# Two places for the queries, half a score tile ahead over ends of blocks, and one place for elu's exponential and h

## The chip, the cores and the metric

The kernel runs on one core of a Trainium2 chip. Its time is the device time of one execution in microseconds (us). Before the change it is 4391.52 us, the median of three executions (4390.94 to 4396.86).

The engines of a core work side by side, each through its own queue in order: TensorE (PE in the profile, its weight loads PEld), VectorE (DVE), ScalarE (ACT), GpSimd (POOL) and SyncE (SP). In this kernel every DMA is issued from SP's queue.

## The reference

Two layers over x of shape (8, 2048, 256), with one adjacency matrix of 2048 x 2048. Layer 0 is attention with 4 heads of 64, whose softmax is taken within each chunk of 256 keys, then an output projection with a residual and a layer norm. Layer 1 is a graph attention whose weights come from two scores per node. Each layer's output is added to its input and normalised. Cut to what matters:

```python
q, k, v = (x @ W.T + b for each)                     # 4 heads of 64
scores = clip(q @ kc.T / 8, -10, 10)                 # for each chunk of 256 keys
scores = where(adj == 0, -10, scores)
ctx = sum over chunks of softmax(scores) @ vc
h = layernorm(x + layernorm(ctx @ Wo.T + bo + x) * gamma + beta)
# layer 1
Wh = h @ W;  e = leaky_relu(Wh @ a1 + (Wh @ a2).T, 0.2)
p = softmax(where(adj > 0 or diagonal, e, -inf))
out = layernorm(h + elu(p @ Wh))
```

## The kernel before, in words

**Blocks, chunks, beats.** Layer 0 works on *blocks* of 512 queries of one batch: 8 batches x 4 blocks = 32. A block goes through 8 *chunks* of 256 keys (j), a chunk through two *beats* (half 0 and 1) of 128 keys, whose number within the block is c (0 to 15). The loop over J (256 chunks and one more) writes out the work of all engines in the order in which each engine's queue will hold it.

**A beat.** The scores of 128 keys and 4 heads are two *halves* (hp), each a tile `sc` of 128 x 1024 in PSUM: four matmuls in the profile (L882), one clip with the mask's cap on VectorE (L893), one exponential on ScalarE (L897) into a tile e. Then come the context's matmuls of the chunk before (L948): in half 0 the sums (weights `ones`) and the first part of the values, in half 1 the second part. Each ends in a tile m of two places in PSUM, which ScalarE copies out (ds L962, un L956). The sums go over SP: dc<-ds (L964), a reciprocal on VectorE (L970), rd<-dc (L972), r<-rd (L976). Two beats later VectorE scales un by r (L983) and POOL adds it to ctxT (L984).

**Halves ahead.** `sc` has two places of its own. While layer 1 is not under way (`spare`), its accumulator's place `us` serves as a third, and each beat multiplies and clips the first half of the *next* beat as well (`todo`, L922 to L933, kept in `ahead_sc`); the next beat begins with its exponential. Before the change this stops at a block's last beat (`c + 1 < NT`).

**Queries.** qT, the block's projected queries, has one place. x's transposed block xT_q is loaded (512 KB, L120) at the end of chunk 6 of the block before (`j == NCH - 2`). At the end of chunk 7 `make_qT` projects it: 8 matmuls pq in the profile (L256) in two m tiles, evicted by ScalarE (L257).

**Ends of beats.** `end_beat` writes out layer 1's products (L746), then one step of each generator: `ahead` (a batch's prelude of layer 1, with pw L398, psj L416, the maxima L438 and pab L461) and `fins`. The latter hold the keys' and values' projections (pk L256, pv L275), in batch 0 the masks (mk L154 and L155, mb L157, mf L201), `fin` (the output of a layer 0 block: x is loaded, po L357, two layer norms, h stored, transposed by pt L383) and `fin1` (the end of a layer 1 block). Then the agenda's reciprocals and scalings. A generator's `yield` ends its share of the beat.

**Layer 1.** Steps of 128 keys run beside layer 0, 1.5 to a beat: w in five places through ScalarE (L714), VectorE (L718, L723), ScalarE (L727), then its products and on POOL the sum acc (L734, L736). They start a few chunks into a batch, when the prelude is done, so every batch has a stretch without them; batch 0 has none at all.

**fin1.** It loads h (hr, 512 KB, L591), divides by the sums (L597 to L601), takes the exponential ex (L603), builds elu (L605, VectorE), adds hr (L606, POOL), and normalises (`stats`, `normalize`, L611). hr and ex have a place of 4 KB per partition each. `fin1_last` does the same for the last batch, with its own ex. The place of hr also serves un in some chunks of batch 0.

Of the kernel before, what the change touches and what calls it, by code (L numbers as in the profile page):

```python
# [9 lines left out]
F32 = mybir.dt.float32  # L10
# [9 lines left out]
P = 128  # L20
# [8 lines left out]
def tile_adj_attention__then__gat(  # L29
# [35 lines left out]
    nc = tc.nc  # L65
    B, N, F = x.shape
    H, D = 4, 64
    CHUNK = 256
    KC = F // P
    NT = N // P  # L70
    IB = 512
    NIB = N // IB
    TPB = IB // P
    NPAIR = H // 2
    NCH = N // CHUNK
    DH = D // 2
    HT = NT // 2
    HN = N // 2
    QSCALE = 1.0 / D**0.5
# [38 lines left out]
    def xT_tile(b, ib, name):  # L118
        t = four.tile([P, KC, IB], F32, tag="xT", name=f"xT_{name}{b}_{ib}")
        nc.sync.dma_start(out=t, in_=xT[b, :, ts(ib, IB)].rearrange("(k p) n -> p k n", p=P))  # L120
        return t
# [5 lines left out]
    bq_c = load_c("bq_c", bq)  # L127
# [99 lines left out]
    nc.sync.dma_start(out=W_aug[:, :, 0:F], in_=W.rearrange("(k p) o -> p k o", p=P))  # L227
    a_bc = []
    for n in range(2):
        t = one.tile([P, F], F32, tag=("hx", "ex")[n], name=f"a_bc{n}")  # L230
        nc.sync.dma_start(out=t, in_=a[n * F : (n + 1) * F, :].rearrange("f o -> (f o)").partition_broadcast(P))
        a_bc.append(t)

# [17 lines left out]
    def proj_T(dst, name, xt, bias, scale, tag):  # L251

        for o in range(NPAIR):
            pm = ps_m.tile([P, IB], F32, tag="m", name=f"p{tag}_{o}")
            for k in range(KC):
                nc.tensor.matmul(pm, WT[name][:, k, ts(o, P)], xt[:, k, :], start=(k == 0), stop=(k == KC - 1))  # L256
            nc.scalar.activation(dst[:, o, :], pm, AF.Identity, bias=bias[:, o : o + 1], scale=scale)  # L257
# [26 lines left out]
    def projections():  # L284


        for b in range(B):
            first = (b * NIB - 1) * 2 * NCH
            for n in range(NIB):
# [13 lines left out]
                    yield  # L303
                make_v(b, n)

    def make_qT(b, ib, xt):
        qT = one.tile([P, NPAIR, IB], F32, tag="qT", name=f"qT{b}_{ib}")
        proj_T(qT, "q", xt, bq_c, QSCALE, f"q{b}_{ib}")
        return qT

    def stats(src, name):

# [274 lines left out]

    def fin1(b, ib, hx, acc):

        hr = one.tile([P, TPB, F], F32, tag="hr", name=f"hr{b}_{ib}")  # L590
        nc.sync.dma_start(out=hr, in_=h_d[b, ib])  # L591
        yield


        pr = ps_m.tile([P, TPB], F32, tag="m", name=f"pr{b}_{ib}")
        for t in range(TPB):
            nc.tensor.matmul(pr[:, t : t + 1], acc[:, ts(t, P)], ones[:, 0:1], start=True, stop=True)  # L597
        r = two.tile([P, TPB], F32, tag="r1", name=f"r1{b}_{ib}")
        nc.vector.reciprocal(r, pr)
        for t in range(TPB):  # L600
            nc.scalar.activation(hx[:, t, :], hx[:, t, :], AF.Identity, bias=ones[:, 0:1], scale=r[:, t : t + 1])  # L601
        ex = one.tile([P, TPB, F], F32, tag="ex", name=f"ex{b}_{ib}")
        nc.scalar.activation(ex, hx, AF.Exp, bias=shifts[:, 1:2])  # L603
        yield
        nc.vector.scalar_tensor_tensor(hx, ex, 1.0, hx, ALU.min, ALU.max)  # L605
        nc.gpsimd.tensor_add(hx, hx, hr)  # L606
        yield
        mv, rstd = yield from stats(hx, f"c{b}_{ib}")
        yield
        normalize(hx, mv, rstd, f"c{b}_{ib}")  # L610
        nc.sync.dma_start(out=out[b, ts(ib, IB), :].rearrange("(t p) f -> p t f", p=P), in_=hx)  # L611

    def fin1_last(b, ib, hx):


        hr = one.tile([P, TPB, F], F32, tag="hr", name=f"hr{b}_{ib}")
        nc.sync.dma_start(out=hr, in_=h_d[b, ib])
        ex = one.tile([P, TPB, F], F32, tag="ex", name=f"ex{b}_{ib}")
        st = two.tile([P, TPB, 6], F32, tag="st", name=f"st_c{b}_{ib}")
        mv = two.tile([P, TPB, 2], F32, tag="mv", name=f"mv_c{b}_{ib}")  # L620
        rstd = two.tile([P, TPB], F32, tag="rstd", name=f"rstd_c{b}_{ib}")
        nmr = two.tile([P, TPB], F32, tag="nmr", name=f"nmr_c{b}_{ib}")
        ends = ib == NIB - 1

        def exponential(r):
            nc.scalar.activation(ex[:, r, :], hx[:, r, :], AF.Exp, bias=shifts[:, 1:2])

        def elu(r):
            nc.vector.scalar_tensor_tensor(hx[:, r, :], ex[:, r, :], 1.0, hx[:, r, :], ALU.min, ALU.max)

# [12 lines left out]
        def scale(t):  # L643
            nc.scalar.activation(
                hx[:, t, :], hx[:, t, :], AF.Identity, bias=nmr[:, t : t + 1], scale=rstd[:, t : t + 1]
            )

        def store(r):
            n = (r.stop - r.start) * P
            q0 = ib * IB + r.start * P  # L650
            nc.sync.dma_start(out=out[b, q0 : q0 + n, :].rearrange("(t p) f -> p t f", p=P), in_=hx[:, r, :])

        halves = [slice(0, 2), slice(2, 4)]
        if ends:
# [12 lines left out]
        yield  # L667
        for r in halves:
            exponential(r)
            yield  # L670
            elu(r)
        yield
        for r in halves:
            add(r)
            yield
        for t in range(TPB):
            tile_stats(t)
            yield
        spread_of(slice(0, TPB))
        yield  # L680
        for r in halves:
            for t in range(r.start, r.stop):
                scale(t)
            yield
        store(slice(0, TPB))
# [176 lines left out]
    blocks0 = {(0, 0, 0): first_m0}  # L862
    make_kT(0, 0)
    make_mask(0, first_m0, first_raw, 0, 0, 0, 2)
    qT = make_qT(0, 0, xT_kv[0, 0])
    fins.append(projections())
    fins.append(weights_made())
    fins.append(masks_made())
# [3 lines left out]
    halves_done = 0  # L872
    ahead_sc = None

    def scores(n, hp):

        nonlocal halves_done
        pool, tag = (ps_u, "us") if spare and halves_done % 3 == 2 else (ps_s, "sc")
        halves_done += 1
        sc = pool.tile([P, 2, IB], F32, tag=tag, name=f"sc{b}_{ib}_{n}_{hp}")  # L880
        for h in range(2):
            nc.tensor.matmul(  # L882
                sc[:, h, :],
                kTs[b][n // TPB][h * D : (h + 1) * D, hp, ts(n % TPB, P)],
                qT[h * D : (h + 1) * D, hp, :],
                start=True,
                stop=True,
            )
        return sc

    def clip(sc, n):
        cap = blocks0[b, ib, n // HT][:, n % HT, :].unsqueeze(1).to_broadcast([P, 2, IB])
        nc.vector.scalar_tensor_tensor(sc, sc, -CLIP, cap, ALU.max, ALU.min)  # L893

    def exponentials(chunk, n, hp, sc):
        e = eight.tile([P, 2, IB], F32, tag="e", name=f"e{b}_{ib}_{n}_{hp}")
        nc.scalar.activation(e, sc, AF.Exp)  # L897
        chunk["es"].append(e)

    for J in range(total + 1):  # L900
# [5 lines left out]
        for half in range(2):  # L906
# [11 lines left out]
            if live:  # L918


                spare = not (l1_open() or leaking)
                todo = [(c, hp) for hp in range(0 if ahead_sc is None else 1, NPAIR)]  # L922
                if spare and c + 1 < NT and (b, ib, c + 1) != (0, 0, HT):
                    todo.append((c + 1, 0))
                scs = [scores(n, hp) for n, hp in todo]
                for (n, hp), sc in zip(todo, scs):
                    clip(sc, n)
                ahead_sc = None
                for (n, hp), sc in zip(todo, scs):
                    if n == c:  # L930
                        exponentials(cur, c, hp, sc)
                    else:
                        ahead_sc = sc  # L933
            middle_of_beat()
# [60 lines left out]
            end_beat()  # L995
            if half == 1:

                if live and j == NCH - 2 and J + 2 < total:
                    nb, nib = (b, ib + 1) if ib + 1 < NIB else (b + 1, 0)
                    xq = xT_tile(nb, nib, "q")  # L1000
                if live and j == NCH - 1 and J + 1 < total:
                    qT = make_qT(nb, nib, xq)
            beat += 1
        prev = cur if live else None

# [49 lines left out]
```

## Time and profile before

| what | value |
|---|---|
| median of three executions | 4391.52 us |
| the profiled execution | 4386.54 us |
| its span, first to last instruction | 4384.7 us |
| mean granted TensorE clock | 0.979 |
| TensorE busy | 4055.8 us |
| VectorE busy | 3417.1 us |
| ScalarE busy | 2555.5 us |
| GpSimd busy | 1759.3 us |
| pq matmuls (248 and 8 more in the first block) | 115.8 and 3.6 us busy |
| scores, L882 (4096) | 1038.7 us busy |
| clips, L893 (1024) | 1205.8 us busy, 1.222 us each |

The profile comes from one execution. Its page gives busy times of engines and groups of instructions; other views give who waited for whom, one tile's instructions and their waits, and a timeline. A line of the timeline reads: start, duration, engine, source line, operation, output<-inputs, shapes and xcount, and in brackets the idle time of the engine before it and what ended it. Lines that follow each other on one engine with the same operation are merged. Two matmuls of the program with f32 operands stand as four in the profile. Matmuls are pipelined and their ends are modelled.

### The profile page before, as it was taken

The numbers are of one execution on the slowest core, as the hardware profiler recorded it, in microseconds if no ns is written. First come the engines' busy times: TensorE is split into PE (matmuls) and PEld (weight loads), VectorE is DVE, ScalarE is ACT, GpSimd is POOL, SyncE is SP. The second block draws the span as 40 slices with busy tenths as digits, with TensorE's granted clock in tenths as the row PEclk, the third lists the DMA queues.
The fourth block names the chain that finished last, engine by engine and source line by source line (L and its number), as shares of the span: only waits on it lengthen the run. The fifth ranks groups of instructions, "written<-read, shape, count | busy, mean of one in ns | idle before, by whom it ended". The sixth has DMA issues, their size and how long they took to land.

```text
span 4384.7 us, 61166 instructions
## 1 busy us (share of the span) xinstructions
PE 4055.8 (92%) x23053; PEld 1913.0 (44%) x23053; DVE 3417.1 (78%) x4530; ACT 2555.5 (58%) x3842; POOL 1759.3 (40%) x901
## 2 busy tenths in 40 slices
PE   8889989999899999999899998999989999899767
PEld 3223334454345534454344543445434454344456
DVE  5876589965898668976699766996579965888777
ACT  5655556665566556666566665566556665555546
POOL 0222235543455434444245442554325542354420
PEclk9999999999999999999999999999999999999889
DMA  5554232223332133321333223222232222322321
GB/s 163 172 174 149 73 114 86 84 72 95 93 97 82 56 108 102 100 75 47 108 103 98 74 74 105 83 95 80 72 105 84 89 78 65 117 83 81 123 73 58
DMA packets 257642, 415.63 MB, mean 95 GB/s; under 512 B 85441, under 2 KB 120513, under 8 KB 256449
## 3 DMA queue, kind: packets, MB, share of 16 engines
q1 hardware_dynamic: 257344, 411.71, 30.7%
q8 instruction: 181, 2.97, 0.3%
q14 instruction: 117, 0.95, 0.1%
HBM read 340.66 MB, written 68.88 MB: 93 GB/s over the span
## 4 chain that ended last, share of the span: by engine, by line
PE 57%; DVE 23%; ACT 7%; DMA 7%; issue 5%; POOL 1%; SPq 0%; DVEq 0%; ACTq 0%; POOLq 0%
PE u L948 17%; PE sc L882 14%; PE us L746 12%; DVE sc L893 6%; DVE fb L438 3%; DVE w L718 3%; PE pv L275 3%; PE pk L256 3%; ACT e L897 3%; DMA dc<-ds 2%; PE pq L256 2%; DVE w L723 2%; PE po L357 2%; PE pw L398 2%; PE us L761 1%
## 5 line engine op out<-in xcount | busy, mean ns | idle before, releaser
L893 DVE SCALAR_TENSOR_TENSOR sc<-sc,mk 128x1024 f32<-128x1024 f32 x1024 | 1205.8, 1222 | 523.1 <-PE sc L882 375.0
L897 ACT ACTIVATE e<-sc 128x1024 f32<-128x1024 f32 x1024 | 1032.7, 1021 | 951.8 <-DVE sc L893 926.5
L882 PE MATMUL sc<-qT,kT 64*128 64x512 f32 x4096 | 1038.7, 622 | 71.8 <-ACT e L897 68.6
L984 POOL TENSOR_TENSOR ctxT<-ctxT,un 128x1024 f32<-128x1024 f32 x224 | 567.9, 2535 | 1135.6 <-DVE un L983 1099.8
L948 PE MATMUL u<-e,v 128*32 128x512 f32 x8192 | 982.8, 597 | 0.0
L746 PE MATMUL us<-wh,w 128*128 128x256 f32 x3584 | 883.0, 396 | 89.5 <-ACT w L727 68.2
L746 PEld LDWEIGHTS us<-wh,w 128*128 128x128 f32 x3584 | 669.8, 194 | 432.5 <-ACT w L727 119.7
L736 POOL TENSOR_TENSOR acc<-acc,w 128x512 f32<-128x512 f32 x392 | 600.0, 1531 | 548.1 <-ACT w L727 537.6
L882 PEld LDWEIGHTS sc<-qT,kT 64*128 64x128 f32 x4096 | 344.3, 186 | 581.3 <-issue 313.7
L718 DVE SCALAR_TENSOR_TENSOR w<-ab,sj,w 128x512 f32<-128x512 f32 x512 | 576.5, 1147 | 6.1 <-ACT w L714 6.1
L948 PEld LDWEIGHTS u<-e,v 128*32 128x32 f32 x8192 | 240.6, 110 | 659.8 <-issue 500.9
L948 PE MATMUL u<-e,ones 128*32 128x512 f32 x4096 | 498.4, 605 | 0.0
L723 DVE TENSOR_TENSOR w<-w,mk 128x512 f32<-128x512 f32 x512 | 458.5, 916 | 45.6 <-DMA mk<-mask 43.1
L438 DVE CUSTOM_DVE_ANT_0 fb<-sj_row,fb 128x1024 bf16<-128x1024 f32 x240 | 383.7, 1609 | 4.5 <-DMA fb<-far 4.5
L956 ACT COPY un<-u 128x512 f32<-128x512 f32 x512 | 300.7, 587 | 108.8 <-PE u L948 100.1
L714 ACT ACTIVATE w<-ab,sj 128x512 f32<-128x512 f32 x512 | 352.3, 715 | 9.9 <-POOL acc L734 5.2
L727 ACT ACTIVATE w<-w 128x512 f32<-128x512 f32 x512 | 308.8, 629 | 83.6 <-DVE w L723 83.2
L983 DVE TENSOR_TENSOR un<-un,r 128x1024 f32<-128x1024 f32 x224 | 277.2, 1238 | 43.6 <-DMA r<-rd 23.1
L948 PEld LDWEIGHTS u<-e,ones 128*32 128x32 f32 x4096 | 107.5, 110 | 352.7 <-issue 286.5
L970 DVE RECIPROCAL dc<-dc 128x16 f32<-128x16 f32 x256 | 63.5, 248 | 149.3 <-DMA dc<-ds 137.3
L962 ACT COPY ds<-u 128x512 f32<-128x512 f32 x256 | 148.6, 580 | 18.5 <-PE u L948 15.5
L357 PE MATMUL po<-WT_o,ctxT 128*128 128x256 f32 x512 | 127.4, 405 | 33.3 <-POOL ctxT L984 29.2
(112 smaller groups left out, 3078.7 us busy)
## 6 DMA issues: line engine op xcount, KB each, us to landing
r<-rd SPq DMA_DIRECT2D x256, 256.0 KB
mk<-mask SPq DMA_DIRECT2D x120, 512.0 KB
fb<-far SPq DMA_DIRECT2D x240, 256.0 KB
xT_k<-in_xT_dram SPq DMA_DIRECT2D x32, 512.0 KB
raw<-in_adjT_dram SPq DMA_DIRECT2D x32, 512.0 KB
rawf<-in_adj_dram SPq DMA_DIRECT2D x32, 512.0 KB
x<-in_x_dram SPq DMA_DIRECT2D x32, 512.0 KB
h_d<-y SPq DMA_DIRECT2D x32, 512.0 KB
```

What stands on the lines that cost most here:

```text
L438: nc.vector.tensor_tensor_reduce(out=fb, in0=row, in1=fb, scale=1.0, scalar=2 * FAR * 0.999, op0=ALU.add, op1=ALU.max, accum_out=dst,)
L714: nc.scalar.activation(self.w, k["ab"][:, 1, :], AF.Identity, bias=k["sj"][:, 1, c : c + 1])
L718: nc.vector.scalar_tensor_tensor(self.w, k["ab"][:, 0, :], k["sj"][:, 0, c : c + 1], self.w, ALU.add, ALU.max)
L723: nc.vector.tensor_tensor(self.w, self.w, self.k["mks"][self.c // HT][:, self.c % HT, :], ALU.min)
L727: nc.scalar.activation(self.w, self.w, AF.Exp)
L736: nc.gpsimd.tensor_add(k["acc"], k["acc"], self.w)
L746: nc.tensor.matmul(k["us"][:, t, :], self.w[:, ts(t, P)], k["wh"][c // TPB][:, c % TPB, 0:F], start=(first and t % 2 == 0), stop=last, ski ...
L882: nc.tensor.matmul(sc[:, h, :], kTs[b][n // TPB][h * D : (h + 1) * D, hp, ts(n % TPB, P)], qT[h * D : (h + 1) * D, hp, :], start=True, sto ...
L893: nc.vector.scalar_tensor_tensor(sc, sc, -CLIP, cap, ALU.max, ALU.min)
L897: nc.scalar.activation(e, sc, AF.Exp)
L948: nc.tensor.matmul(m[h * DH : (h + 1) * DH, :], prev["v"][pc // TPB][:, pc % TPB, f0 : f0 + DH] if part < 2 else ones[:, 0:DH], prev["es"] ...
L984: nc.gpsimd.tensor_add(p["ctxT"], p["ctxT"], p["un"])
```

## The change

1. qT gets two places (pool `two`). xT_q is loaded at the end of chunk 5 instead of chunk 6, and projected at the end of chunk 6 instead of chunk 7. The next block's indices are kept as `nxt`.
2. `scores` and `clip` take batch and block as arguments, and a block's last beat may take the next block's first half ahead, under the same condition `spare`.
3. ex in `fin1` takes the place of hr. h is loaded there only behind L605, which reads ex, and one more beat passes (`yield`) before the add. ex in `fin1_last` takes the place of `fin`'s x, and the second half of a, broadcast at the start, takes the place of y.

```diff
-        t = one.tile([P, F], F32, tag=("hx", "ex")[n], name=f"a_bc{n}")
+        t = one.tile([P, F], F32, tag=("hx", "y")[n], name=f"a_bc{n}")
...
+    qTs = {}
+
     def make_qT(b, ib, xt):
-        qT = one.tile([P, NPAIR, IB], F32, tag="qT", name=f"qT{b}_{ib}")
-        proj_T(qT, "q", xt, bq_c, QSCALE, f"q{b}_{ib}")
-        return qT
+        qTs[b, ib] = two.tile([P, NPAIR, IB], F32, tag="qT", name=f"qT{b}_{ib}")
+        proj_T(qTs[b, ib], "q", xt, bq_c, QSCALE, f"q{b}_{ib}")
...
     def fin1(b, ib, hx, acc):
-        hr = one.tile([P, TPB, F], F32, tag="hr", name=f"hr{b}_{ib}")
-        nc.sync.dma_start(out=hr, in_=h_d[b, ib])
         yield
...
-        ex = one.tile([P, TPB, F], F32, tag="ex", name=f"ex{b}_{ib}")
+        ex = one.tile([P, TPB, F], F32, tag="hr", name=f"ex{b}_{ib}")
         nc.scalar.activation(ex, hx, AF.Exp, bias=shifts[:, 1:2])
         yield
         nc.vector.scalar_tensor_tensor(hx, ex, 1.0, hx, ALU.min, ALU.max)
+        hr = one.tile([P, TPB, F], F32, tag="hr", name=f"hr{b}_{ib}")
+        nc.sync.dma_start(out=hr, in_=h_d[b, ib])
+        yield
         nc.gpsimd.tensor_add(hx, hx, hr)
...
-        ex = one.tile([P, TPB, F], F32, tag="ex", name=f"ex{b}_{ib}")
+        ex = one.tile([P, TPB, F], F32, tag="x", name=f"ex{b}_{ib}")
...
-                todo = [(c, hp) for hp in range(0 if ahead_sc is None else 1, NPAIR)]
-                if spare and c + 1 < NT and (b, ib, c + 1) != (0, 0, HT):
-                    todo.append((c + 1, 0))
+                todo = [(b, ib, c, hp) for hp in range(0 if ahead_sc is None else 1, NPAIR)]
+                if spare and 2 * J + half + 1 < 2 * total and (b, ib, c + 1) != (0, 0, HT):
+                    todo.append((b, ib, c + 1, 0) if c + 1 < NT else (*nxt, 0, 0))
...
+                if live and j == NCH - 3 and J + 3 < total:
+                    nxt = (b, ib + 1) if ib + 1 < NIB else (b + 1, 0)
+                    xq = xT_tile(*nxt, "q")
                 if live and j == NCH - 2 and J + 2 < total:
-                    nb, nib = (b, ib + 1) if ib + 1 < NIB else (b + 1, 0)
-                    xq = xT_tile(nb, nib, "q")
-                if live and j == NCH - 1 and J + 1 < total:
-                    qT = make_qT(nb, nib, xq)
+                    make_qT(*nxt, xq)
```

More of the change, by code (lines that the diff above doesn't have):

```diff
@@ L864, in tile_adj_attention__then__gat @@
     make_mask(0, first_m0, first_raw, 0, 0, 0, 2)
-    qT = make_qT(0, 0, xT_kv[0, 0])
+    make_qT(0, 0, xT_kv[0, 0])
     fins.append(projections())
@@ L873, in tile_adj_attention__then__gat, with scores @@
     ahead_sc = None
-    def scores(n, hp):
+    def scores(b, ib, n, hp):
         nonlocal halves_done
@@ L884, in scores @@
                 kTs[b][n // TPB][h * D : (h + 1) * D, hp, ts(n % TPB, P)],
-                qT[h * D : (h + 1) * D, hp, :],
+                qTs[b, ib][h * D : (h + 1) * D, hp, :],
                 start=True,
@@ L889, in scores, with clip @@
         return sc
-    def clip(sc, n):
+    def clip(sc, b, ib, n):
         cap = blocks0[b, ib, n // HT][:, n % HT, :].unsqueeze(1).to_broadcast([P, 2, IB])
@@ L921, in tile_adj_attention__then__gat @@
                 spare = not (l1_open() or leaking)
-                todo = [(c, hp) for hp in range(0 if ahead_sc is None else 1, NPAIR)]
-                if spare and c + 1 < NT and (b, ib, c + 1) != (0, 0, HT):
-                    todo.append((c + 1, 0))
-                scs = [scores(n, hp) for n, hp in todo]
-                for (n, hp), sc in zip(todo, scs):
-                    clip(sc, n)
+                todo = [(b, ib, c, hp) for hp in range(0 if ahead_sc is None else 1, NPAIR)]
+                if spare and 2 * J + half + 1 < 2 * total and (b, ib, c + 1) != (0, 0, HT):
+                    todo.append((b, ib, c + 1, 0) if c + 1 < NT else (*nxt, 0, 0))
+                scs = [scores(*which) for which in todo]
+                for which, sc in zip(todo, scs):
+                    clip(sc, *which[:3])
                 ahead_sc = None
-                for (n, hp), sc in zip(todo, scs):
-                    if n == c:
-                        exponentials(cur, c, hp, sc)
+                for which, sc in zip(todo, scs):
+                    if which[2] == c:
+                        exponentials(cur, c, which[3], sc)
                     else:
```

## The prediction

> **What bounds the kernel now.** I read the page first, then TensorE's own waits, then the stretches around the ends of blocks in the timeline.
>
> ```profile
> PE 4055.8 (92%) x23053; PEld 1913.0 (44%) x23053; DVE 3417.1 (78%) x4530; ACT 2555.5 (58%) x3842; POOL 1759.3 (40%) x901
> ```
>
> TensorE (PE) is busy 92% of the span of 4384.7 us, and 329 us are left in which it is not. The change adds and removes no matmul, so it can only win or lose in those 329 us, or in the clock. TensorE's waits, longest in total first (us, times, longest):
>
> ```profile
> PE sc L882 <- ACT e L897: 68.6, 53, 4.9
> PE us L746 <- ACT w L727: 68.2, 44, 10.8
> PE po L357 <- POOL ctxT L984: 29.2, 14, 4.3
> ...
> PE pq L256 <- ACT un L956: 10.4, 12, 0.9
> PE pq L256 <- DMA xT_q<-in_xT_dram: 8.6, 3, 3.9
> ```
>
> Only the last two rows belong to the queries' projection (pq): 10.4 + 8.6 = 19.0 us, in 15 places. No row has TensorE waiting for the evicted queries (ACT qT). The view of tile pq lists only the weight load (PEld) as doing so, which runs beside matmuls:
>
> ```profile
>   ACT qT L257: 87.8, 55
>   PEld sc L882: 17.5, 32
> ```
>
> Both rows are idle time that is covered: ScalarE waits 87.8 us for pq, and 17.5 us in 32 times is 0.55 us of a weight load. Now one end of a block without layer 1 (batch 2, first block to second), TensorE alone:
>
> ```profile
> 1072.33 1.13 PE L882 MATMUL sc<-qT,kT 64*128 64x512 f32 x4
> 1073.39 1.92 PE L948 MATMUL u<-e,v 128*32 128x512 f32 x16
> 1075.25 0.28 PE L416 MATMUL psj<-ident,sj 128*16 128x128 f32 x1
> 1076.40 3.70 PE L256 MATMUL pq<-xT_q,WT_q 128*128 128x512 f32 x8 [0.88 <-ACT un L956]
> 1080.03 2.85 PE L882 MATMUL sc<-qT,kT 64*128 64x512 f32 x12
> ```
>
> The block's last beat has 4 score matmuls (half a tile; the other half was ahead), the next block's first has 12. From pq on TensorE goes straight into the scores: the first half of qT is evicted while pq's second half is multiplied. So the visible hole, "no half ahead over the end", costs VectorE idle time, not TensorE time:
>
> ```profile
> 1081.26 3.49 DVE L893 SCALAR_TENSOR_TENSOR sc<-sc,mk 128x1024 f32<-128x1024 f32 x3 [6.45 <-PE sc L882]
> 1084.67 1.22 DVE L983 TENSOR_TENSOR un<-un,r 128x1024 f32<-128x1024 f32 x1
> 1087.94 0.25 DVE L970 RECIPROCAL dc<-dc 128x16 f32<-128x16 f32 x1 [2.06 <-issue]
> ```
>
> VectorE stood 6.45 us and had three clips at once, but at 1085.9 it had caught up and waited for the small dc transfer. A clip earlier buys nothing behind that point.
>
> **The change part by part.**
>
> *Which ends get the half ahead.* I counted score matmuls around pq at all 31 ends: 11 have the pattern 4 then 12 (the four ends of batch 0, and the first end of batches 1 to 7), 20 have 8 then 8, because layer 1 holds the place. Beats, not times, decide this, so 11 it stays. At these, 4 matmuls (half of 8 at 1.99, less the switch: 2.85 + 1.13 = 3.98 = 2 x 1.99) go one beat earlier: cost and gain 0.0 by themselves.
>
> *pq and its load one chunk earlier.* 31 x 3.70 us of TensorE work, 62 evictions of 0.69 us on ScalarE and 31 loads of 512 KB move; none is added. The extra place for qT is paid by the place that ex gives up. pq's own waits:
>
> (a) Batches 1 to 7, first end: 7 waits of 0.87 to 0.88 us, 6.1 us. There the psj transpose takes one of the two PSUM places (m), so pq must wait for un's copy, which stands behind the last beat's exponential. One chunk earlier the neighbours are pw (four evictions of 0.37 us that keep up), and the beat has 8 score matmuls, 0.86 us more cover. I take all 6.1 as gained; the bounds are 0 and 6.1.
>
> (b) Batch 0, three ends: TensorE waits for the load.
>
> ```profile
> 113.92 0.53 SPq L120 DMA_DIRECT2D xT_q<-in_xT_dram  x1
> ...
> 122.41 5.37 PE L256 MATMUL pq<-xT_q,WT_q 128*128 128x512 f32 x8 [3.90 <-DMA xT_q<-in_xT_dram]
> ```
>
> The three loads landed 8.35, 7.92 and 7.49 us after issue, TensorE stood 3.9 + 2.9 + 1.8 = 8.6. The load keeps one chunk of lead, but chunk 6 is longer than chunk 7: in the first block it holds pv (3.72 us), in the next two pt (1.4), and all get the 0.86 us of scores. In the first block the load would issue at about 100.2 (behind the mask stores at 99.19 and 99.67), landing near 108.6, and pq would be reached at 110.0: no wait. In the second, issue near 206, landing 213.8, reached at 213.1: 0.7. The third alike (issue 307, landing 314.5, reached 314.7). ScalarE may then hold pq's second half back by under 1 us. I take 7 of the 8.6 as gained; the bounds are 0 (load traffic as now) and 8.6.
>
> (c) The clock. The granted clock was 0.72 in 122 to 128 us, after the 3.87 us stand, and pq took 5.37 us instead of 3.70: 1.7 us that go with the stand. The Trainium skill (TensorE: Matmul & The Clock Gate, "Part 1: The HAM clock gate") has the clock halved after an idle window of some 3.4 us, the windows running freely. That speaks against counting on the 1.7, since another phase can put a slow stretch elsewhere; by it the sum would hold 0 here instead of 1.7.
>
> (d) Of the 20 other ends 5 wait 0.85 us (second end of batches 1 to 5), 15 nothing. With layer 1 beside it chunk 6 is no different: 0, bounds -4.3 and +4.3.
>
> Sum for pq: 6.1 + 7 + 1.7 = 14.8 us gained.
>
> *elu and h in one place.* In 28 fin1 runs the load of h comes two stages later, behind L605, and the add (L606, 2.85 us), the statistics and the normalising one beat later. 21 of the 28 have layer 1 behind them.
>
> On SP's queue the load waits for L605 on VectorE. Behind it stand rd and r of the same beat, whose reciprocal comes after L605 on VectorE anyway, and dc of the next beat, whose copy follows exponentials that need clips behind L605. Nothing is held longer: 0, at worst 0.4 us of issue time.
>
> On POOL the add may now wait for the load, with acc adds and ctxT behind it:
>
> ```profile
> 1264.85 2.84 POOL L606 TENSOR_TENSOR hx<-hx,hr 128x1024 f32<-128x1024 f32 x1 [1.23 <-DVE hx L605]
> 1267.64 1.72 POOL L736 TENSOR_TENSOR acc<-acc,w 128x512 f32<-128x512 f32 x1
> 1275.26 1.93 POOL L322 TENSOR_TENSOR rstd_c<-rstd_c,nhalf 128x4 f32<-128x4 f32 x1 [5.90 <-DVE rstd_c L321]
> 1277.17 2.35 POOL L984 TENSOR_TENSOR ctxT<-ctxT,un 128x1024 f32<-128x1024 f32 x1
> ```
>
> Loads of 512 KB of this kind (x, mk) took 3.9 to 8.3 us where something waited for them. Issued at 1264.8, h lands between 1268.7 and 1273.1; the add ends by 1276.0, before ctxT at 1277.2, and POOL stood idle there. So 0, with 1.2 us to spare in the worst case. The Trainium skill (DMA: Bandwidth & Descriptors, "Rules for kernel authors") says to issue a DMA early and wait for it late, which speaks against this edit; by it each add would cost a landing time, which this row of POOL has idle.
>
> The burst of statistics (4 x 0.58 on VectorE) and normalising (4 x 0.59 on ScalarE) lands in beats of the other parity. 28 shifts, each up to about 0.5 us of TensorE's waits either way: 0, bounds -5 and +5. L606 slows a two-input VectorE operation beside it now (two L718 took 3.54 us beside it, 1.41 later); it does so one beat later too.
>
> *Place of a_bc, of ex in the last batch.* Both reuse a place long free; 4 and 8 instructions, 0.
>
> **Sum.** The profiled execution took 4386.54 us (span 4384.7 and 1.8 around it), 5.0 below the median of 4391.52. I round 14.8 down to 14, for a wait that reappears elsewhere: 4391.5 - 14 = 4377.5 us.
>
> **The rivals.**
>
> *The gain is taken back* (23%): TensorE arrives earlier, and meets the next wait. After the 11 ends, in the block's second chunk, stand 46 us of TensorE idle time (sc for e, po for ctxT) set by VectorE's mask and far work and dc's landing. If they grow by what pq loses, 5 us or less stay: about 4387. For it: in batch 0 VectorE was busy 12.96 of the 13 us from 240 to 253. Against it: between those waits TensorE runs full for 10 us and more.
>
> *Those waits shrink too* (15%): the clip taken early frees 1.2 us on VectorE at each end. In batch 0's first end VectorE runs without a break from 128.95 to 139.8 and TensorE's 0.76 us wait hangs on it. If a third of the 46 goes as well, 4377.5 - 15 = 4362. Against it: the wait for dc, above.
>
> *Slower* (12%): h lands late, POOL's queue stands, acc adds release w late, layer 1's next w (five places) waits. It decides when h takes over 9.5 us (8.3 + 1.2), or where POOL's next work follows L605 sooner than the 12.4 us of the rows above; each of 21 adds would then cost about one acc add, 1.5 us: +32, minus the 14: about 4410. Against it: the longest landing seen is 8.3 us.
>
> *The half ahead does not happen* (under 1%): only if layer 1's pace changed.
>
> **How the numbers follow.** Forecast 50%, taken back 23%, waits shrink 15%, slower 12%. The bounds of the forecast are 20.7 gained (6.1 + 8.6 + 1.7 + 4.3) and, with 5 us left of pq's gain and the ends of (d), the shifts and the issue time against it, 5 - 4.3 - 5 - 0.4 = 4.7 lost: 4371 to 4396. The range reaches down to the shrinking waits, 4362, and leaves out the slower rival and some 5% below: 4362 to 4396. A measurement tells 0.2%, 8.8 us, from no change. Faster by more: nine tenths of the forecast and the shrinking waits, 45 + 15 = 60%. Within: the rest of the forecast and the gain taken back, 5 + 23 = 28%. Slower: 12%.
>
> **What would show it.** In the profile after: "PE pq <- DMA xT_q" gone or under 2 us, "PE pq <- ACT un" down from 10.4 to about 4; 8 and 8 score matmuls at all ends; VectorE's 6.45 us stand gone; L606 waiting for a DMA instead of L605, and TensorE's "us <- ACT w" at 68 as before. It is wrong if that last row or "sc <- ACT e" grows by over 10 us, or if pq still waits in its new place.

## The result, and the profile after

The changed kernel takes 4413.3 us (median of six executions, 4409.7 to 4417.9) beside 4392.2 us for the kernel before on the same chip (4388.4 to 4396.9): a ratio of 1.0048 [1.0038, 1.0058]. The forecast was 4377.5 us; 4413 lies outside its range. The profiled execution after took 4415.6 us, its span 4413.8, at a mean granted clock of 0.973 (before: 4384.7 and 0.979).

The page's first row and TensorE's waits after (us, times, longest):

```profile
PE 4075.4 (92%) x23053; PEld 1927.2 (44%) x23053; DVE 3387.8 (77%) x4530; ACT 2563.5 (58%) x3842; POOL 1743.3 (39%) x901
```

```profile
PE sc L884 <- ACT e L899: 84.2, 56, 4.9
PE us L748 <- ACT w L729: 75.4, 43, 8.9
PE pab L462 <- ACT ds L964: 39.1, 21, 3.2
...
PE po L358 <- POOL ctxT L986: 21.0, 8, 3.6
PE pt L384 <- ACT ds L964: 16.4, 10, 2.5
...
PE pq L256 <- ACT un L958: 3.9, 4, 1.4
...
PE pq L256 <- DMA xT_q<-in_xT_dram: 0.5, 1, 0.5
```

pq's own waits fell from 19.0 to 4.4 us, as forecast. But TensorE is busy 19.6 us longer with the same 23053 matmuls, at a lower mean clock, and other waits grew: sc for e by 15.6 us, pab for ds by 20.3 (it was 18.8), us for w by 7.2; po fell by 8.2 and pt by 8.3.

The end shown before the change (batch 2, first block to second), TensorE alone, after:

```profile
1079.48 0.28 PE L417 MATMUL psj<-ident,sj 128*16 128x128 f32 x1
1079.69 1.99 PE L884 MATMUL sc<-qT,kT 64*128 64x512 f32 x8
...
1088.95 1.13 PE L884 MATMUL sc<-qT,kT 64*128 64x512 f32 x4
1094.08 1.13 PE L884 MATMUL sc<-qT,kT 64*128 64x512 f32 x4 [4.01 <-ACT e L899]
1095.14 3.57 PE L950 MATMUL u<-e,ones 128*32 128x512 f32 x16
...
1107.76 5.41 PE L358 MATMUL po<-WT_o,ctxT 128*128 128x256 f32 x16 [3.56 <-POOL ctxT L986]
```

pq is gone from this stretch and the scores go 8 and 8, as said. Two new things are seen: TensorE stands 4.01 us, and the next 16 sums take 3.57 us instead of 1.92 (the granted clock was 0.50 from 1095.1 to 1098.5). VectorE and SP's queue there show why:

```profile
1083.75 1.22 DVE L985 TENSOR_TENSOR un<-un,r 128x1024 f32<-128x1024 f32 x1 [0.45 <-DMA r<-rd]
1091.60 0.25 DVE L972 RECIPROCAL dc<-dc 128x16 f32<-128x16 f32 x1 [6.62 <-DMA dc<-ds]
1091.77 2.33 DVE L895 SCALAR_TENSOR_TENSOR sc<-sc,mk 128x1024 f32<-128x1024 f32 x2
```

```profile
1080.37 0.33 SPq L421 DMA_DIRECT2D sj_d<-sjr  x1
1083.82 0.34 SPq L422 DMA_DIRECT2D sj_row<-sj_d  x1
1084.21 0.90 SPq L431 DMA_DIRECT2D fb<-far  x2
1085.15 0.63 SPq L347 DMA_DIRECT2D x<-in_x_dram  x1
1085.88 0.56 SPq L966 DMA_DIRECT2D dc<-ds  x1
```

The stand of 6.45 us that VectorE had before its three clips is gone, and one of 6.62 us before the reciprocal stands in its place: dc, 8 KB, is issued 0.7 us behind a burst of 2 MB (sj_row 1 MB, two fb of 256 KB, x 512 KB) and takes 5.7 us. The clips behind the reciprocal are late, and e, and TensorE. Before, SP's queue stood thus:

```profile
1080.26 0.33 SPq L421 DMA_DIRECT2D sj_row<-sj_d  x1
1080.65 0.90 SPq L430 DMA_DIRECT2D fb<-far  x2
1081.59 0.70 SPq L346 DMA_DIRECT2D x<-in_x_dram  x1
1085.45 0.56 SPq L964 DMA_DIRECT2D dc<-ds  x1
```

pq lay between psj and the scores, so dc came 3.9 us behind the burst, and was there at 1087.9.

Seven waits of VectorE like that one for dc, 6.2 to 7.1 us each, stand in the trace after, one at the first end of each of batches 1 to 7; before, none there is over 4.23 us.

Two stands of TensorE followed in the block's second chunk before the change, too:

```profile
1098.47 1.13 PE L882 MATMUL sc<-qT,kT 64*128 64x512 f32 x4 [1.71 <-ACT e L897]
...
1104.44 3.72 PE L357 MATMUL po<-WT_o,ctxT 128*128 128x256 f32 x16 [2.99 <-POOL ctxT L984]
```

### The profile page after: what moved, and what is told of

Its sections match the earlier page's. It is cut to its first block, busy times and chain, and to the rows that moved or that the text cites. A ratio compares the mean times of both kernels' runs of the same rounds, so it can differ in the third digit from the quotient of the medians.

```text
span 4413.8 us, 61162 instructions
## 1 busy us (share of the span) xinstructions
PE 4075.4 (92%) x23053; PEld 1927.2 (44%) x23053; DVE 3387.8 (77%) x4530; ACT 2563.5 (58%) x3842; POOL 1743.3 (39%) x901
## 4 chain that ended last, share of the span: by engine, by line
PE 65%; DVE 17%; ACT 6%; DMA 6%; issue 5%; POOL 1%; SPq 1%; DVEq 0%; ACTq 0%; POOLq 0%
PE u L950 20%; PE sc L884 15%; PE us L748 15%; DVE sc L895 4%; PE pk L256 3%; PE po L358 3%; PE pv L275 2%; PE pw L399 2%; PE pq L256 2%; DMA dc<-ds 2%; DVE fb L439 2%; DVE w L720 2%; ACT e L899 2%; DVE w L725 2%; PE us L763 1%
## 5 line engine op out<-in xcount | busy, mean ns | idle before, releaser
L884 PE MATMUL sc<-qT,kT 64*128 64x512 f32 x4096 | 1046.6, 627 | 87.5 <-ACT e L899 84.2
L738 POOL TENSOR_TENSOR acc<-acc,w 128x512 f32<-128x512 f32 x392 | 594.7, 1517 | 565.0 <-ACT w L729 555.1
L720 DVE SCALAR_TENSOR_TENSOR w<-ab,sj,w 128x512 f32<-128x512 f32 x512 | 538.5, 1073 | 17.2 <-ACT w L716 17.1
L950 PE MATMUL u<-e,ones 128*32 128x512 f32 x4096 | 508.7, 615 | 0.0
L725 DVE TENSOR_TENSOR w<-w,mk 128x512 f32<-128x512 f32 x512 | 420.4, 842 | 44.0 <-DMA mk<-mask 41.4
L439 DVE CUSTOM_DVE_ANT_0 fb<-sj_row,fb 128x1024 bf16<-128x1024 f32 x240 | 393.6, 1650 | 3.3 <-DMA fb<-far 3.3
L985 DVE TENSOR_TENSOR un<-un,r 128x1024 f32<-128x1024 f32 x224 | 294.5, 1315 | 52.4 <-DMA r<-rd 49.9
L350 POOL TENSOR_TENSOR y<-x,bo_bc 128x1024 f32<-128x1024 f32 x32 | 79.4, 2480 | 201.2 <-DMA x<-in_x_dram 130.6
```

Source lines behind the costliest of these rows:

```text
L439: nc.vector.tensor_tensor_reduce(out=fb, in0=row, in1=fb, scale=1.0, scalar=2 * FAR * 0.999, op0=ALU.add, op1=ALU.max, accum_out=dst,)
L720: nc.vector.scalar_tensor_tensor(self.w, k["ab"][:, 0, :], k["sj"][:, 0, c : c + 1], self.w, ALU.add, ALU.max)
L725: nc.vector.tensor_tensor(self.w, self.w, self.k["mks"][self.c // HT][:, self.c % HT, :], ALU.min)
L738: nc.gpsimd.tensor_add(k["acc"], k["acc"], self.w)
L884: nc.tensor.matmul(sc[:, h, :], kTs[b][n // TPB][h * D : (h + 1) * D, hp, ts(n % TPB, P)], qTs[b, ib][h * D : (h + 1) * D, hp, :], start=True,
L950: nc.tensor.matmul(m[h * DH : (h + 1) * DH, :], prev["v"][pc // TPB][:, pc % TPB, f0 : f0 + DH] if part < 2 else ones[:, 0:DH], prev["es"] ...
```

## The experiments

How far a kernel runs behind the one before (+) or ahead of it (-) is read from the start of the same chunk's first sums in both traces, in us:

| at the start of | change | fin1 alone | queries alone | seven ends as before | batch 0 only | fin1, a beat more |
|---|---|---|---|---|---|---|
| batch 1 | -8.5 | +4.5 | -7.3 | -8.2 | -7.6 | +1.6 |
| batch 2 | +0.6 | +8.4 | +1.0 | -5.7 | -6.3 | -2.1 |
| batch 4 | +13.8 | +11.2 | +4.4 | -6.2 | -8.8 | -12.7 |
| batch 7 | +33.1 | +19.9 | +16.8 | -2.0 | -5.2 | -23.4 |
| end of span | +29.1 | +14.4 | +17.8 | -1.4 | -2.7 | -36.6 |

Batch 0 gains 8 us wherever its queries are early; what is lost is lost from batch 1 on. The table is of single executions; the ratios below are of several.

**Fin1's edit alone** (before, with the edit of `fin1` in item 3 only: no `fin1_last`, no queries').

> The kernel before with the edit of fin1 alone (ex in the place of h, h loaded behind L605, one more beat before the add); the queries as before. Theory A: the extra beat brings fin1's statistics into the beat of fin's statistics in the last block of batches 1 to 6, VectorE has 4.6 us of them in a row, the clips and with them the copy of the sums come late, and TensorE stands 3.15 us at pab with 3.4 us of half clock behind it; with the step at the block's start before it that is some +33 us, so about 4425 us (4415 to 4432), with the 3.15 us waits at pab in the trace. Rival R1, the loss belongs to the queries' edits: 4392 us, no long wait at pab. Rival R2, h lands late and holds POOL: slower as well, but with acc adds behind L606 and w's places short, and no wait at pab.

Measured: 1.0007 [0.9998, 1.0016], 4388.9 beside 4385.3 us. Its profiled execution was the slowest of twelve (4382.8 to 4400.9). In sum fin1's edit costs nothing that can be told, but not for the reason that the prediction gave: its trace holds six stands of pab of 3.15 to 3.16 us that were not there, and gains elsewhere. So the stands of theory A are there, and its 33 us are not.

**The added beat taken back** (after, without fin1's first `yield`: pr, ex and L605 a beat earlier, the statistics in the beat of before).

```diff
     def fin1(b, ib, hx, acc):
-        yield
```

> The changed kernel without fin1's first yield: h still comes late and ex keeps the shared place, but the statistics are back in the beat that they had before; the sums' matmuls pr come one beat earlier. Theory A: the 33 us go, about 4380 us (4374 to 4388), pab waits 0.9 us as before. R1: 4413 us. R2: still slower, 4405 us or more, since h comes as late as in the changed kernel and the add still waits for it.

Measured: 1.0119 [1.0106, 1.0132]. Worse. In this trace two of VectorE's w (L724) take 4.76 us at 1341.6, beside `fin`'s two additions of x on GpSimd; then elu (L605 before, L603 here), un and ctxT are late, ScalarE waits 6.91 us for acc (L735) until 1354.5, and TensorE stands 3.5 us. Such a wait of ScalarE, 6.9 to 8.4 us, stands once in each of batches 1 to 6. TensorE's sc for e waits are 106.3 us (change: 84.2). That this is all of the loss is not shown.

**dc from ScalarE's queue** (after, dc of the chunk at those seven ends), and **both** (with the run above).

```diff
+                        own = nc.scalar if prev["b"] > 0 and prev["ib"] == 0 and prev["j"] == NCH - 1 else nc.sync
-                        nc.sync.dma_start(
+                        own.dma_start(
```

> The changed kernel, with the dc transfer of seven beats (first beat of the second block of batches 1 to 7) issued from ScalarE's queue instead of SyncE's; all else alike. Theory B: at these ends dc stands behind sj_row, two fb and x (2.5 MB) in one queue, since pq no longer lies between psj and the sums; on a queue of its own it lands in 2 to 3 us instead of 5.7, VectorE's wait of 6.2 to 7.1 us falls under 3.5 us, TensorE's 3.6 to 4.1 us wait for a score place goes, and about 20 us (14 to 30) come back: 4393 us. Rival R3, the 16 engines themselves are full and dc is late on any queue: 4413 us, the wait stays over 5 us. Rival R4, the wait is there but TensorE's loss is not from it: the wait falls, the time stays within 5 us of 4413.

> Both edits of the two runs before together. Theories A and B, which lie in different blocks of a batch, add up: 4413 - 33 - 20 = 4360 us (4350 to 4374), faster than both kernels. If they are one cause, or give way to the next wait: no lower than the better of the two alone.

Measured: 1.0035 [1.0022, 1.0048] and 1.0100 [1.0086, 1.0114]. Two lines of ScalarE's and VectorE's timeline of the first of these, at the same end:

```profile
1082.75 0.55 ACTq L967 DMA_DIRECT2D dc<-ds  x1
```

```profile
1089.37 0.25 DVE L973 RECIPROCAL dc<-dc 128x16 f32<-128x16 f32 x1 [6.45 <-issue]
```

Issued from another queue, while SP was issuing the two fb (1082.34) and ahead of x (1083.28), dc took 6.6 us all the same (the profile names no releaser of the reciprocal here, but it is the reader of dc; at the six other ends VectorE waits 5.3 to 6.6 us for dc). What holds it is not its place in SP's queue; the burst that moves at the same time is left, and the run with the burst later, below, bears that out. The Trainium skill (DMA: Bandwidth & Descriptors, "Issuing engines are not separate DMA queues") says that DMAs of all issuing engines run on the same 16 engines and interleave, and these rows agree.

**No half ahead over ends** (after, with `c + 1 < NT` put back).

> The changed kernel without the half ahead over ends of blocks (c + 1 < NT as before); the queries stay two-placed and one chunk early, fin1 stays changed. Theory C: the half ahead moves no TensorE time, the loss at the first ends of batches 1 to 7 comes from pq's leaving alone; as slow as the changed kernel, ratio to before 1.003 to 1.006, with VectorE's waits of 6 us for dc in the trace. Rival R5, the half ahead is what costs (VectorE and the score places are a half further at the wrong moment): the ratio falls to 1.001 or under.

Measured: 1.0054 [1.0041, 1.0067]. Within the intervals the half ahead over ends is neither loss nor gain; the loss does not need it.

**The burst a beat later** (after, sj_row and the first two fb behind dc).

```diff
...
-        key_rows(b, sj, sj_row, slice(0, NT))
+        row_load = key_rows(b, sj, sj_row, slice(0, NT), later=True)
...
+        yield
+        row_load()
         fbs, fb_load = far_loads(b, [(it, hf) for it in range(NT) for hf in range(2)])
-        yield
         yield
```

> The changed kernel with sj_row and the first two fb loads (2 MB) issued one beat later, behind that beat's dc instead of ahead of it; psj, the copy and the store of sj_d stay, and the first use of fb keeps its beat. Theory B (dc is late because the burst fills the engines, whatever the queue): dc's waits of 6 to 7 us at the seven ends fall to 3 us or less, TensorE's stands of 3.3 to 4.1 us there go with the half clock behind them, about 25 us come back (15 to 35): ratio to before 0.997 to 1.002. Rival R4: the waits fall, the time does not (1.004 and more), because VectorE's work behind it is the bound there. Rival R6: sj_row now lands late and VectorE stands for it at the first maximum instead.

Measured: 1.0038 [1.0024, 1.0051]. VectorE's waits for dc are all under 3.6 us now, and the kernel is as slow as without this edit, within the intervals: TensorE's waits of po for ctxT grew from 21.0 to 43.5 us. By the start times the loss behind these ends comes one chunk later and is nearly as large.

**The queries' edits alone** (after, with fin1 as before. To find room, ex is bf16 in a place of its own and ds has one place), and **the same with the burst later**.

> The queries' edits alone: two places, pq one chunk early, the half ahead; fin1 in its beats of before, with ex in a place of its own. To find room ex is bf16 (elu's negative side is rounded) and ds has one place; neither is on the path that sets the end. With fin1's edit alone at +3 us, the queries' edits should carry nearly all of the loss: ratio 1.003 to 1.005, no 3.15 us waits at pab, but dc's 6 us waits. Rival R7, the two parts only cost together (the stands of the one move the other's beats): 1.000 or under here.

> The queries' edits alone and the burst one beat later, the two runs before taken together. If theory B is right and pq's old waits (19 us idle) stay gone, this is the gain that was forecast, 10 to 20 us: ratio 0.996 to 0.998, faster than both kernels. If other stands take the freed time: 1.000.

Measured: 1.0039 [1.0026, 1.0052] and 1.0033 [1.0020, 1.0046]. The two parts add up: 0.0007 + 0.0039 = 0.0046, against 0.0048. In the second VectorE waits for the burst itself instead of dc, as its timeline at the end of batch 2 shows:

```profile
1087.63 2.58 DVE L445 CUSTOM_DVE_ANT_0 fb<-sj_row,fb 128x1024 bf16<-128x1024 f32 x1 [1.83 <-DMA fb<-far]
...
1096.41 1.23 DVE L445 CUSTOM_DVE_ANT_0 fb<-sj_row,fb 128x1024 bf16<-128x1024 f32 x1 [2.77 <-DMA fb<-far]
```

So it is not dc's wait alone. Read from these traces, the whole chain from psj to po sets this stretch: sj out and back, the burst, dc, rd, r, the maxima (L438) and ctxT. Which link weighs most was not taken apart; whether TensorE's own work sets it, the next run asks.

**A filler in pq's old place** (queries alone, with eight matmuls of pq's shape, whose product nothing reads, at the seven ends). If the chain sets the stretch, they must be free.

```diff
+                if live and j == NCH - 1 and b > 0 and ib == 0:
+                    for o in range(NPAIR):
+                        pm = ps_m.tile([P, IB], F32, tag="m", name=f"fill{b}_{o}")
+                        for k in range(KC):
+                            nc.tensor.matmul(
+                                pm, WT["q"][:, k, ts(o, P)], kTs[b][0][:, k, :], start=(k == 0), stop=(k == KC - 1)
+                            )
```

> The queries' edits alone (ratio 1.0039) with work added: at the end of the last beat of the first block of batches 1 to 7, where pq used to be, 8 matmuls of pq's shape whose result nobody reads, 3.7 us each time, 7 times. Theory D: from psj to po at these ends the transfers (sj_row, fb, x, dc, rd, r), VectorE's maxima and ctxT set the length, and pq was free in it; the filler costs nothing, ratio 1.0025 to 1.0050, with shorter TensorE stands and less half clock. Rival R8, TensorE sets the length there: 7 x 3.7 = 26 us more, ratio 1.0098.

Measured: 1.0043 [1.0030, 1.0057], span 4402.9 us, where the queries alone have 1.0039 and 4402.5. Seven times 3.7 us, 26 us of TensorE, cost nothing. VectorE's waits for dc at these ends are 3.5 us at the most there, and that gains nothing either. Its TensorE at the end of batch 2:

```profile
1074.99 0.28 PE L417 MATMUL psj<-ident,sj 128*16 128x128 f32 x1
1075.77 3.70 PE L1008 MATMUL fill<-kT,WT_q 128*128 128x512 f32 x8 [0.50 <-ACT un L957]
...
1102.85 5.41 PE L358 MATMUL po<-WT_o,ctxT 128*128 128x256 f32 x16 [3.49 <-POOL ctxT L985]
```

From psj to po it is 27.9 us with the filler; with the queries alone 27.8 (1080.46 to 1108.23), with the change 28.3, and before, with pq in it, 29.2 (1075.25 to 1104.44). TensorE's work in this stretch is cover, not cost. pq cost nothing there; one chunk earlier it costs its 3.7 us, and this stretch gives back 0.9 to 1.4. The start times say the same: in the change's trace each of the seven ends is 3.4 us longer in the chunk that pq has come to, 4.6 shorter in the one that it has left, and 3.0 to 5.1 longer in the chunk after that.

**The seven ends as before** (queries alone, but at these ends load, projection and first half at their old places).

```diff
-                if spare and 2 * J + half + 1 < 2 * total and (b, ib, c + 1) != (0, 0, HT):
+                late = b > 0 and ib == 0
+                if spare and (c + 1 < NT or not late) and 2 * J + half + 1 < 2 * total and (b, ib, c + 1) != (0, 0, HT):
...
+                late = b > 0 and ib == 0
-                if live and j == NCH - 3 and J + 3 < total:
+                if live and j == NCH - 3 + late and J + 3 - late < total:
...
-                if live and j == NCH - 2 and J + 2 < total:
+                if live and j == NCH - 2 + late and J + 2 - late < total:
```

> The queries' edits alone, but at the seven first ends of batches 1 to 7 the load, pq and the scores stand as in the kernel before (pq behind the last beat, no half ahead). Theory D: the 26 us that the trace shows at these ends go, and pq's old wait of 0.87 comes back 7 times: 17.8 - 25.9 + 8.2 (what the trace shows at chunk 7) = 0, ratio 0.9985 to 1.0012. Rival R9, the loss is spread over all ends: 1.003 and more.

**Batch 0 only** (before, with early queries and the half ahead at the ends of batch 0 alone; the second place for qT is ex's, idle in batch 0).

> The kernel before, with the queries' edits at the four ends of batch 0 alone (the second place of qT is the one of ex, which batch 0 does not use; fin1 as before). There pq's wait for its load goes and nothing of layer 1 stands behind it: the trace of the changed kernel is 7 to 8 us ahead when batch 0 ends and that should stay, ratio 0.9982 (0.9972 to 0.9992). Rival R10, the lead is lost again in batch 1: 1.000.

Measured: 0.9993 [0.9984, 1.0002] and 0.9978 [0.9969, 0.9987]. The first takes away 0.0046 of the queries' 1.0039, all of their loss: it sits at the seven ends, 19.2 us by the spans (4402.5 - 4383.3), 2.7 each. The second keeps batch 0's gain, 9.6 us.

**Fin1 with a beat more** (fin1 alone, with one `yield` between the add of h and the statistics).

```diff
         nc.gpsimd.tensor_add(hx, hx, hr)
+        yield
         yield
         mv, rstd = yield from stats(hx, f"c{b}_{ib}")
```

> The kernel before with fin1's edit alone (ratio 1.0007) and one beat more between the add and the statistics, so that they leave the beat of fin's statistics. Theory A: TensorE's 3.15 us stands at pab go (six of them, with half clock behind), ratio 0.997 to 1.0000. Rival R11, they are only put elsewhere: the stands at pab go, the ratio stays at 1.0005 and more.

Measured: 0.9915 [0.9901, 0.9928], 4350.6 us, far below both kernels. Where fin1's edit loses is seen at the third end of batch 2. TensorE before, then after, then with the beat more:

```profile
1374.12 0.27 PE L461 MATMUL pab<-ident,m 128*8 128x128 f32 x1 [0.90 <-ACT ds L962]
1374.60 3.70 PE L256 MATMUL pk<-xT_k,WT_k 128*128 128x512 f32 x8 [0.21 <-ACT un L956]
```

```profile
1380.58 0.27 PE L462 MATMUL pab<-ident,m 128*8 128x128 f32 x1 [3.16 <-ACT ds L964]
1381.07 5.40 PE L256 MATMUL pk<-xT_k,WT_k 128*128 128x512 f32 x8 [0.21 <-ACT un L958]
```

```profile
1368.31 0.27 PE L461 MATMUL pab<-ident,m 128*8 128x128 f32 x1 [0.83 <-ACT ds L964]
1368.80 3.70 PE L256 MATMUL pk<-xT_k,WT_k 128*128 128x512 f32 x8 [0.21 <-ACT un L958]
```

And VectorE after the change, just ahead:

```profile
1370.66 0.42 DVE L317 BATCH_NORM_STATS2 st_a<-y 128x6 f32<-128x256 f32 x1
...
1372.98 0.42 DVE L317 BATCH_NORM_STATS2 st_c<-hx 128x6 f32<-128x256 f32 x1
...
1376.64 2.35 DVE L895 SCALAR_TENSOR_TENSOR sc<-sc,mk 128x1024 f32<-128x1024 f32 x2
```

The beat that fin1 got puts its statistics (st_c) right behind those of `fin` (st_a): eight in a row from 1370.7 to 1375.2, with the clip, e and the copy ds behind them. TensorE stands 3.16 us for pab, and pk runs at a granted clock of 0.63 (1380.9 to 1384.3): 2.3 + 1.7 us. It happens in the last block of batches 1 to 6, six times 3.15 to 3.17 us, and by the start times each costs about 5 us (there the change goes from +4.6 to +9.7). One beat more, and the two sets of statistics no longer meet, the clips stand between them:

```profile
1360.72 0.42 DVE L316 BATCH_NORM_STATS2 st_a<-y 128x6 f32<-128x256 f32 x1
...
1364.37 2.35 DVE L895 SCALAR_TENSOR_TENSOR sc<-sc,mk 128x1024 f32<-128x1024 f32 x2
...
1367.91 0.42 DVE L316 BATCH_NORM_STATS2 st_c<-hx 128x6 f32<-128x256 f32 x1
```

But the kernel before has no such collision either (0.90 us at pab), so this explains the loss against the run with the beat more, and not why that run is faster than the kernel before.

**The rest of it.** Four more runs asked whether the parts are separate, and whether the statistics' beat is all of that gain: the whole change with the beat more; the same with early queries in batch 0 alone (`late = b > 0` in the diff above, the half ahead over ends there too); before with two beats more ahead of the statistics, h loaded early; and before with one beat more ahead of the add of h and one ahead of the statistics, h loaded early.

> The whole change, with one beat more in fin1 between the add of h and the statistics. If fin1's beat and the queries' places cost and gain separately (the change alone 1.0048, fin1 alone 1.0007, fin1 with one beat more 0.9915): 1.0048 - 0.0092 = 0.9956, about 4372 beside a before of 4391, and fewer than two stands of pab behind ds over 3 us per batch. If the loss at the seven first ends is of one kind with the colliding statistics (both a late ds), it goes as well: 0.992. If the two collide in new ways: above 0.998.

> As the run before it, but queries are taken early, and half a tile goes ahead over ends of blocks, in batch 0 alone; the ends of batches 1 to 7 are as before the change. If the gains add (0.9978 for batch 0 alone, 0.9915 for fin1 with one beat more): 0.9893, about 4344 beside 4391. If batch 0's gain is taken back once the rest of the program shifts: 0.9915.

> Before the change, with two beats more in fin1 between the add of h and the statistics; h is loaded as early as before, and no place is shared. If the gain of fin1 with one beat more comes from the beat of the statistics and the normalising alone: 0.9915, as there. If half of it comes from h's later load or the later add: about 0.995. If all of it does: 1.000 or above.

> Before the change, with one beat more in fin1 between elu's L605 and the add of h and one more between the add and the statistics; h is loaded as early as before, and no place is shared. It has the add and the statistics in the beats of the run in which fin1 alone got one beat more (0.9915), without the late load. Two of that run's four tenths of a per cent beyond the run with late statistics alone (0.9953) sit, by the traces, in stands of pt behind ds: the add runs on GpSimd beside L718 there, two of which then take 3.54 us instead of 1.40. If the beat of the add is all of the rest: 0.991 to 0.992, stands of pt behind ds about 15 us instead of 24. If the late load of h is: 0.995.

Measured: 0.9958 [0.9946, 0.9970], 0.9902 [0.9887, 0.9916], 0.9953 [0.9939, 0.9966] and 0.9920 [0.9906, 0.9934]. The first is the sum that was forecast for separate parts, 0.9956. The second, 4344.4 us beside 4385.8, has the lowest ratio of all; it agrees with its sum, 0.9893, but its interval reaches 0.9915 as well, so it doesn't tell whether batch 0's gain is kept there. Of fin1's gain, 0.0047 comes from the beat of the statistics, 0.0033 more from the beat of the add, and the late load of h gives nothing that can be told (0.9915 against 0.9920). How the later statistics gain is not shown: with them alone no single wait of TensorE accounts for it; po for ctxT falls by 7.8 us, pw for un by 5.5, us for w by 4.2 and its busy time by 6.5, while po for un grows by 3.6.

How the add's beat matters is seen at the prediction's own row of GpSimd: at 1264.85 L606 ran 2.84 us. VectorE beside it before, then after, where the add runs at 1273.76:

```profile
1264.70 3.54 DVE L718 SCALAR_TENSOR_TENSOR w<-ab,sj,w 128x512 f32<-128x512 f32 x2
```

```profile
1268.09 1.40 DVE L720 SCALAR_TENSOR_TENSOR w<-ab,sj,w 128x512 f32<-128x512 f32 x2
...
1274.03 3.38 DVE L985 TENSOR_TENSOR un<-un,r 128x1024 f32<-128x1024 f32 x1
```

The 2.1 us that the add takes from VectorE fall on L718 before, ahead of two clips, and TensorE's pt then waits 1.75 us for ds; after, they fall on un's scaling, 1.22 us alone, behind the clips. With the later add TensorE's pt for ds is 16.4 us after and in the last run

```profile
PE pt L383 <- ACT ds L964: 14.5, 9, 1.9
```

against 24.7 before and 24.4 with late statistics alone. The Trainium skill (SBUF — State Buffer, "SBUF: two separate sides") has VectorE's instructions with two inputs in SBUF and GpSimd's that read SBUF exclude each other for a whole instruction on a shared port; the rows agree for L718 and L985, and for the clips, one of whose inputs is in PSUM: after the change two took 2.35 us at 1269.42 beside GpSimd's L738 (1269.80), and the same elsewhere.

## Why the prediction was wrong, point by point

- **pq's waits** (a, b): right that they go; 10.4 to 3.9 and 8.6 to 0.5 us. **Batch 0** is right in time too: 7 and 1.7 were forecast, 9.6 measured (0.9978), and the first pq there takes 3.67 us instead of 5.37.
- **(a), the step that failed:** "31 x 3.70 us of TensorE work ... move; none is added", with 6.1 us taken as gained at seven ends. The work isn't added, but the cover it gave is lost: in its old place, at those ends, it lay beside a chain of transfers that ends at po, and cost nothing (the filler: 26 us for nothing); in its new place it costs. Measured -19.2 us (queries alone against the seven ends as before), where +6.1 stood. The prediction read the old stretch as TensorE's own, since "from pq on TensorE goes straight into the scores"; but two stands followed in the same stretch, 1.71 us for e and 2.99 for ctxT, a sign that something else set its end.
- **The rival "taken back"** named the right place, those 46 us of waits of "sc for e, po for ctxT" and dc's landing, and its bound was wrong: it let them grow by what pq loses in waits, not by pq itself.
- **(c):** the 1.7 us came (behind a stand of 3.90 us by its row, where the prediction wrote 3.87), and more was lost than that elsewhere: TensorE's busy time grew by 19.6 us, as the mean granted clock fell from 0.979 to 0.973.
- **(d):** 0, by the spans (seven ends as before against batch 0 only: 1.3 us apart); by the ratios 0.0015 or 6.6 us lost, with intervals that overlap, and the first of the two also has ex in bf16 and one place for ds. **The half ahead:** 0 was right (1.0054 without it, 1.0048 with it).
- **elu and h.** SP's queue: nothing speaks against 0. The add of h waits for its load now, 48.9 us in 11 times, 8.8 at the longest, and that costs nothing that can be told (0.9915 with the late load, 0.9920 without): the slower rival's mechanism did not decide. But "the burst of statistics ... in beats of the other parity: 0, bounds -5 and +5" was an unsupported guess: one beat costs six collisions of 5 us, a beat further they are gone, and with the statistics alone two beats later 0.0047 is gained, some 20 us, against a kernel that had no collision. And "L606 slows a two-input VectorE operation beside it now; it does so one beat later too" missed which one: there nobody soon waits for it, and pt gains 8 us. That losses and gains cancelled to 1.0007 was luck, not a zero; pt's 8 us are only part of the gains, and the rest was not traced.
- **Signals.** It was to be wrong if sc for e grew by over 10 us; it grew by 15.6. The forecast sum, -14, became +21: queries about -9.6 in batch 0 and +20 at the seven ends (0.0039 - (-0.0007) is 0.0046), the other ends +7 at the most (d), and fin1's edit about +4 (1.0048 - 1.0039).

Open is why fin1's profiled execution ran 14 us behind while its median is 3.6 behind; its executions spread over 18 us, and where slow stretches of the clock fall may differ between them, which was not traced.

## What to carry to other kernels

Before you move work of the busiest engine, ask what sets the end of the stretch that it leaves and of the one that it enters; "the engine is 92% busy" answers neither. A filler of the same shape in the old place tells it in one run: if it is free, the work was cover, and taking it away gives little back there. And a beat in a hand-made order has no price of its own: look at what stands in the beat it shifts into, on every engine, and try the next beat too; here the change's own fin1 edit gained nothing with one added beat and 37 us with two.

## What the runs showed of the hardware

- **The clock.** In the trace after, the six stands of 3.15 to 3.17 us at pab were each followed by a lower granted clock (0.50 to 0.66 over the next 3.4 us), and pk took 5.25 to 5.40 us instead of 3.70. A stand of 2.99 us was followed by a full-speed po (3.72 us for 16 matmuls) in the trace before and by a slow one (5.32) in the run without the half ahead. In the run with dc from ScalarE's queue a stand of 3.28 us was followed by full speed:

```profile
1091.86 1.13 PE L884 MATMUL sc<-qT,kT 64*128 64x512 f32 x4 [3.28 <-ACT e L899]
1092.91 1.92 PE L950 MATMUL u<-e,ones 128*32 128x512 f32 x16
```

So a little more waiting can cost 1.7 us on top, and the length of a stand near 3 us does not tell alone whether it does. The Trainium skill (TensorE: Matmul & The Clock Gate, "Part 1: The HAM clock gate") puts the idle window at some 3.4 us, free-running; here shorter stands were followed by slow stretches, at some places and not at others.
- **A small transfer behind a burst.** 8 KB took 5.7 us when issued 0.7 us behind the last of 2 MB, from SP's queue, and 6.6 us amid them, from ScalarE's; before, issued 3.9 us behind the same burst, at most 2.5 (1085.45 to the reciprocal at 1087.94).
